# Q, K and softmax sums in four 64x64 quadrants on two PSUM banks, in a kernel of convolution, attention and experts

## The chip, the cores and the metric

The kernel runs on one core of a Trainium2 chip. A core has five engines that each work through their own instructions in order and wait for one another by semaphores: TensorE (PE, matrix products; its weight loads are shown apart as PEld), VectorE (DVE), ScalarE (ACT), GpSimd (POOL) and SyncE (SP, which issues most transfers). Matrix products go to PSUM, a small memory of eight banks of 2 KB in each of 128 partitions; ScalarE and VectorE carry them from there to SBUF.

The metric is the device time of one execution in microseconds (us). Before the change three runs took 1254.31 to 1254.89 us, median 1254.82.

## The reference, cut to what matters

Two layers on an input of 2 images, 256 channels, 56 x 56 pixels (N = 3136 tokens each). The first is a linear non-local convolution. The second is a transformer block on the tokens, all in float32:

```python
qkv = x @ W_attn                              # x: layer-normed tokens, C = 256
q, k, v = split(qkv)                          # 4 heads of 64
att = q @ k.T / 8, causal                     # per head, 3136 x 3136
att = softmax(att)
y = att @ v
t = t + y @ W_proj
t = t + experts(layernorm(t))                 # top 2 of 8 experts, 256 -> 512 -> 256
```

The change lies in the causal attention: in how Q and K are made, in how the rows of exponentials are summed for the softmax, and in when other work is put between the attention's steps.

## The kernel before

The program first does the convolution (to about 95 us), then the attention of both images (batches) in one long list of steps (to about 843 us), then the experts.

**Steps.** A step (`attend`, L707) belongs to a batch b, a block i of W = 448 queries (seven blocks), a head pair hp (two pairs, hp 0 first) and a chunk j of 128 keys. `scores` (L779) makes the products of keys and queries, transposed: keys in partitions, queries in columns, a 64x64 quadrant of the array for each half of the chunk and each head of the pair, into a tile `sc` of two banks, one for each head. ScalarE writes the exponentials to a tile `st` (L808; five buffers), VectorE multiplies the chunks that the causal mask cuts (L811) and adds `st` to the accumulator `acc` (L822 for a group's first two steps, L827 after). `values` (L832) runs three steps later (`LAG`) and adds the products with V to the output tile `yp`, two banks, a single buffer. Chunks that the mask cuts have fewer columns; they alternate with whole ones, so a group in block 0 has only narrow steps, block 1 ends on a narrow one, later blocks end on a whole one.

In each turn of the loop at L929 the order on TensorE is: the values of step n - 3, then the scores of step n; but where step n - 3 is the first of its group, its values come after the scores (`late`), so that the one output tile can be emptied. When a group's last values are done, ScalarE copies the output tile (L862) and GpSimd adds its two halves into `qT` (L863).

**Visits.** Three turns after a group's last step (in the turn in which its last values run) there is a visit (L930), ahead of that turn's values. `visit` (L2141) runs pieces that need the full 128x128 array: for hp 0, the Q and K products of the next segment of tokens (`query_key`, L607: two pairs of heads, Q and K, two matmuls of 128x512 each, then a ScalarE copy, L621), projections of finished tokens (`products`, `project_out`, L671), and a transposed tile of normed tokens (`transpose`, L591) of the segment after that; for hp 1 the V products of the next segment and further transposes. Segments have 512 tokens, the last two 384 and 192. These pieces take their PSUM tiles in turn (`bank`, L523) from two single banks (`pm`) and the two score tiles. After them `sum_rows` (L866) sums the accumulator over the keys with a matrix of ones, in four column groups of 32 (128x32 mode, 224 columns each), into a single bank; ScalarE copies the result (L881), four small DMAs on SP's queue write it to memory and one reads it back spread over partitions. Four steps later VectorE takes the reciprocal (`invert`, L892), it goes to memory and back as a broadcast, and six steps after that VectorE scales the output (`scale`, L907).

**Side work.** Between steps, `between` (L2162) pulls one piece of queued work a step (`pull`, L1970): layer-norm statistics of finished tokens (`closer`, L700), then the routing of batch 0's tokens to experts and their scattering, mostly small VectorE operations and GpSimd's indirect transfers. Nothing reorders this: the lists are written out in the program's order (`manual_schedule`, L2113), so each engine's queue is what the loop above emits.

**Score tiles.** `psc` has two buffers of two banks, called A and B here. Every score takes the next one; a score n + 2 thus waits until the exponential of score n has read its tile.

Of the kernel before, what the change touches and what calls it, by code (L numbers as in the profile page):

```python
# [28 lines left out]
def conv_attn_moe_kernel(  # L29
# [481 lines left out]
    def layer1(nm, general):  # L511

        with ExitStack() as whole:
# [20 lines left out]

            def centre_gate(place):

                gp = place("gp", (P, 512))
                gpc = gp[:, :E]
                for c in range(NH):
                    nc.tensor.matmul(gpc, ones, gw[:, c], start=(c == 0), stop=(c == NH - 1))  # L540
                for c in range(NH):
                    nc.vector.scalar_tensor_tensor(gwc[:, c], gpc, -1.0 / C, gw[:, c], ALU.mult, ALU.add)
                    nc.vector.tensor_copy(
                        wv[:, c, :, HS:], gwc[:, c].rearrange("p (h e) -> p h e", h=HEADS)
                    )
# [24 lines left out]
            def project_qkv(b, qT, kT, v, px):  # L570
# [51 lines left out]

                def value(s, n):
# [43 lines left out]
                return xs, qks, vs  # L667
# [30 lines left out]
            unclosed = [NCH] * B  # L698

            def closer(b, first, m, k):  # L700

                for n in range(first, first + m):
                    stats(b, n, 1, k, bg, f"o{nm}{b}")
                    unclosed[b] -= 1
                    yield True

            def attend(qT, kT, v, fst, fs, psc, py, open_batch, visit, between, clock, later, finished):  # L707
# [158 lines left out]
                def sum_rows(b, hp, i):  # L866
                    yh = qT[:, hp, i * W : (i + 1) * W]
                    r = (b * NH + hp) * NB + i
                    sn = f"{nm}{b}_{hp}_{i}"
                    acc = accs[b, hp, i]  # L870
                    summed.add((b, hp, i))
                    sp = bank(f"sp_{b}_{hp}_{i}")

                    flat = acc.rearrange("p a w -> p (a w)")
                    for g in range(4):
                        nc.tensor.matmul(  # L876
                            sp[g * 32 : (g + 1) * 32, : W // 2], ones[:, :32],
                            flat[:, g * W // 2 : (g + 1) * W // 2], start=True, stop=True,
                        )
                    line = fs.tile([P, W], F32, tag="rb", bufs=3, name=f"line_{sn}")  # L880
                    nc.scalar.copy(line[:, : W // 2], sp[:, : W // 2])  # L881
                    halves = sum_d[r].rearrange("a (h w) -> (a h) w", h=2)
                    for g in range(4):
                        nc.sync.dma_start(
                            out=halves[g : g + 1], in_=line[g * 32 : g * 32 + 1, : W // 2]
                        )
                    nc.sync.dma_start(
                        out=sums[:, r], in_=sum_d[r].rearrange("a (p f) -> (a p) f", p=HS)
                    )
                    later.append((clock[0] + 4, invert, b, hp, i, yh))  # L890

                def invert(b, hp, i, yh):  # L892
# [12 lines left out]
                    later.append((clock[0] + 6, partial(scale, rb), b, hp, i, yh))  # L905

                def scale(rb, b, hp, i, yh):  # L907
                    nc.vector.tensor_tensor(yh, yh, rb, ALU.mult)
                    later.append((clock[0] + 2, hand_on, b, hp, i, yh))
# [4 lines left out]
                def due(now):  # L914
                    while later and (now is None or later[0][0] <= now):
                        _, task, b, hp, i, yh = later.pop(0)
                        task(b, hp, i, yh)
                        later.sort(key=lambda e: e[0])

# [9 lines left out]
                for n in range(len(steps) + LAG):  # L929
                    if n in visits:  # L930
                        visit(*visits[n])
                        b, i, hp = visits[n]
                        if i >= 0 and visits[n] != final:
                            sum_rows(b, hp, i)
                        aligned()
                    if n + 1 < len(steps) and n > LAG and steps[n][2] == 0 and steps[n - LAG - 1][2] == 0 and steps[n - LAG - 1][4]:
                        turn_rows(*steps[n][:2])
                    if n < len(steps):
                        b, i = steps[n][:2]
                        if n == 0 or steps[n - 1][0] != b:  # L940
                            open_batch(b)
                        between(b, i, ends[b, i] - n, (steps[n][3] + 1) * P > i * W + 1)
# [5 lines left out]
                    if n >= LAG and not late:  # L948
                        values(n - LAG)
                    if n < len(steps):  # L950
# [3 lines left out]
                sum_rows(final[0], final[2], final[1])  # L954
# [1118 lines left out]
            if general:  # L2073
                centre_gate(bank)
                fold_gate(bank, turn_gate(bank))
                for b in range(B):
                    xs, qks, vs = project_qkv(b, qT, kT, v, px)
# [8 lines left out]
            else:  # L2086
# [9 lines left out]
                def ahead(b, i, hp):  # L2096

                    xs, qks, vs = projections[b]
                    if i < 0:
                        return vs(0), xs(1)  # L2100
                    if i + 1 < NS:
                        if hp == 0:
                            return qks(i + 1), xs(i + 2)[:1]
                        after = projections[b + 1][0](0) if i + 2 == NS and b + 1 < B else []
                        return vs(i + 1), xs(i + 2)[1:] + after
                    if b + 1 == B:
                        return [], []
                    xs, qks, vs = projections[b + 1]
# [5 lines left out]
                xs, qks, vs = projections[0]  # L2114
# [26 lines left out]
                def visit(b, i, hp):  # L2141

                    now, then = ahead(b, i, hp)
# [12 lines left out]
                    for _ in range(2):  # L2156
# [3 lines left out]
                    ring.clear()  # L2160

                def between(b, i, left, cut):  # L2162
# [7 lines left out]
                    if not cut or i:  # L2170
# [262 lines left out]
```

## Time and profile before

| | |
|---|---|
| median of three runs | 1254.82 us |
| the profiled execution | 1272.23 us |
| its span, first to last instruction | 1270.5 us |
| granted TensorE clock, mean | 0.995 |
| TensorE busy | 1247.3 us |
| VectorE busy | 773.9 us |
| ScalarE busy | 613.1 us |
| GpSimd busy | 356.2 us |
| Q and K products (L613), TensorE | 88.2 us, 224 records |
| scores (L804) and values (L855), TensorE | 347.5 and 328.0 us |

How to read it: a float32 matmul shows as two records, each with a weight load. Busy time of TensorE includes the time in which a record's results still move through the array, so a busy TensorE is not one that streams columns all the time; where starts of successive records are known, their distance is the better measure. In a timeline a row is a run of like instructions: start in us from the span's start, length, engine, line, operation, output and inputs, shape, count, and in brackets the idle time before it and who ended it. "64*64" or "128*32" is the part of the array that a matmul uses. A row of the waits names who waited for whom, total us, times and longest.

### The profile page before, as it was taken

The numbers are of one execution on the slowest core, as the hardware profiler recorded it, in microseconds if no ns is written. First come the engines' busy times: TensorE is split into PE (matmuls) and PEld (weight loads), VectorE is DVE, ScalarE is ACT, GpSimd is POOL, SyncE is SP. The second block draws the span as 40 slices with busy tenths as digits, with TensorE's granted clock in tenths as the row PEclk, the third lists the DMA queues.
The fourth block names the chain that finished last, engine by engine and source line by source line (L and its number), as shares of the span: only waits on it lengthen the run. The fifth ranks groups of instructions, "written<-read, shape, count | busy, mean of one in ns | idle before, by whom it ended". The sixth has DMA issues, their size and how long they took to land.

```text
span 1270.5 us, 28742 instructions
## 1 busy us (share of the span) xinstructions
PE 1247.3 (98%) x10881; PEld 857.1 (67%) x10881; DVE 773.9 (61%) x1687; ACT 613.1 (48%) x1237; POOL 356.2 (28%) x318
## 2 busy tenths in 40 slices
PE   8999999999999999999999999999999999999998
PEld 8876655555454645655555543469888999899996
DVE  2683567566766575576677887785743433455664
ACT  0255555565656565455555655563332333344442
POOL 1103231110021104211112766100266112666651
PEclk9999999999999999999999999999999999999999
DMA  9995101000000000100000223641344343466654
GB/s 314 354 345 187 25 23 37 25 15 26 14 17 16 7 20 17 36 21 14 9 16 25 71 67 110 202 136 61 101 135 151 101 114 101 142 200 200 212 164 125
DMA packets 118723, 125.66 MB, mean 99 GB/s; under 512 B 27223, under 2 KB 108488, under 8 KB 118578
## 3 DMA queue, kind: packets, MB, share of 16 engines
q1 hardware_dynamic: 107922, 97.19, 25.3%
q0 software_dynamic: 9840, 25.67, 6.0%
q8 instruction: 90, 1.47, 0.5%
q10 hardware_dynamic: 816, 0.88, 0.2%
q14 instruction: 55, 0.45, 0.1%
HBM read 62.06 MB, written 61.05 MB: 97 GB/s over the span
## 4 chain that ended last, share of the span: by engine, by line
PE 91%; DVE 4%; DMA 1%; issue 1%; ACT 1%; SPq 0%; DVEq 0%; ACTq 0%
PE sc_f L804 19%; PE yp_f L855 18%; PE ht_f L1637 14%; PE yp_f L1656 14%; PE qk_f L613 7%; PE v_f L628 4%; PE pp_f L682 3%; PE cp L410 3%; PE gram L317 2%; DVE acc_f L827 2%; PE tp_f L1614 2%; PE sp_f L876 1%; PE xp_f L599 1%; PE yo_f L1883 1%; DMA w1s_f<-in_w_dram 0%
## 5 line engine op out<-in xcount | busy, mean ns | idle before, releaser
L808 ACT ACTIVATE st_f<-sc_f 128x896 f32<-128x896 f32 (+5 forms) x400 | 330.7, 838 | 198.0 <-PE sc_f L804 178.9
L827 DVE TENSOR_TENSOR acc_f<-acc_f,st_f 128x896 f32<-128x896 f32 (+6 forms) x344 | 344.5, 1002 | 118.9 <-ACT st_f L808 109.1
L804 PE MATMUL sc_f<-qT_f,kT_f 64*64 64x448 f32 (+5 forms) x3136 | 347.5, 499 | 0.3 <-ACT st_f L808 0.3
L855 PE MATMUL yp_f<-st_f,v_f 64*64 64x448 f32 (+5 forms) x2928 | 328.0, 510 | 4.1 <-ACT acc_f L862 2.5
L804 PEld LDWEIGHTS sc_f<-qT_f,kT_f 64*64 64x64 f32 x3136 | 144.8, 133 | 128.9 <-issue 106.2
L1646 ACT ACTIVATE g_f<-ht_f,b1b 128x128 f32<-128x128 f32 x408 | 116.6, 371 | 227.3 <-PE ht_f L1637 123.4
L855 PEld LDWEIGHTS yp_f<-st_f,v_f 64*64 64x64 f32 x2928 | 125.1, 133 | 132.2 <-issue 99.3
L1637 PE MATMUL ht_f<-xT_f,w_f 128*128 128x128 f32 x1600 | 196.9, 276 | 5.2 <-issue 5.2
L1637 PEld LDWEIGHTS ht_f<-xT_f,w_f 128*128 128x128 f32 x1600 | 193.8, 192 | 9.1 <-issue 4.6
L1501 POOL DMA_INDIRECT x_slots<-xr_f,idx x100 | 120.4, 1204 | 147.0 <-DVE xr_f L1499 77.6
L863 POOL TENSOR_TENSOR qT_f<-acc_f 128x448 f32<-128x448 f32 x26 | 29.6, 1140 | 406.3 <-ACT acc_f L862 406.3
L1625 DVE COPY w_f<-w1s_f 128x1024 f32 x102 | 72.7, 713 | 90.0 <-PE ht_f L1637 34.2
L584 POOL TENSOR_SCALAR xn_f<-t 128x256 f32<-128x256 f32 (+1 forms) x50 | 82.4, 1655 | 129.4 <-DVE t L185 43.6
L1677 POOL DMA_INDIRECT y_tokens<-ys_f,to_f x57 | 59.2, 1038 | 125.2 <-DVE ys_f L1666 102.9
L613 PE MATMUL qk_f<-px_f,wat 128*128 128x512 f32 (+2 forms) x224 | 88.2, 546 | 0.6 <-ACT px_f L605 0.6
L1666 DVE TENSOR_TENSOR ys_f<-yp_f,kT_f 128x128 f32<-128x128 f32 x102 | 29.5, 289 | 92.3 <-PE yp_f L1656 69.5
L613 PEld LDWEIGHTS qk_f<-px_f,wat 128*128 128x128 f32 x224 | 40.6, 190 | 46.3 <-issue 41.7
L1656 PE MATMUL yp_f<-px_f,g_f 128*128 x204 | 62.3, 387 | 1.6 <-issue 1.6
L1656 PE MATMUL yp_f<-kT_f,g_f 128*128 x204 | 62.1, 386 | 0.0
L1656 PE MATMUL yp_f<-v_f,g_f 128*128 x204 | 61.8, 385 | 0.0
L1656 PE MATMUL yp_f<-w2s_f,g_f 128*128 x204 | 61.6, 384 | 0.0
L1834 POOL DMA_INDIRECT y_f<-y_slots,idx x50 | 55.5, 1110 | 17.1 <-issue 17.1
(299 smaller groups left out, 1302.4 us busy)
## 6 DMA issues: line engine op xcount, KB each, us to landing
x_slots<-fill SPq DMA_DIRECT2D x1, 8190.0 KB
xb_f<-x_slots SPq DMA_DIRECT2D x60, 130.0 KB
x_slots<-fill SPq DMA_DIRECT2D x1, 7296.0 KB
y_slots<-ys_f SPq DMA_DIRECT2D x57, 128.0 KB
kept<-t SPq DMA_DIRECT2D x2, 3200.0 KB
x<-in_x_dram SPq DMA_DIRECT2D x14, 448.0 KB
rb_f<-inverses SPq DMA_DIRECT2D x56, 112.0 KB
y_f<-y_tokens SPq DMA_DIRECT2D x23, 256.0 KB
```

The source lines that it names most:

```text
L584: nc.gpsimd.tensor_scalar(xn[:k, a], ts[b][:k, n + a, :C], ts[b][:k, n + a, MEAN : MEAN + 1], ts[b][:k, n + a, RSTD : RSTD + 1], ALU.subtr ...
L613: nc.tensor.matmul(ps[:, :w], wat[:, c, d0 : d0 + P], px[:, s % 2, c, :w], start=(c == 0), stop=(c == NH - 1),)
L804: nc.tensor.matmul(to, left, right, start=True, stop=True)
L808: nc.scalar.activation(st[rows, :, c0:], ps[rows, :, c0:W], AF.Exp, scale=SCALE)
L827: nc.vector.tensor_tensor(acc[rows, :, c0:], acc[rows, :, c0:], st[rows, :, c0:], ALU.add)
L855: nc.tensor.matmul(to, left, right, start=first, stop=end)
L1501: s = nc.gpsimd.indirect_dma_start(out=xds[b], out_offset=bass.IndirectOffsetOnAxis(ap=idxs[b][:kk, k, n : n + 1], axis=0), in_=xr[:kk], i ...
L1625: nc.vector.tensor_copy(w, w1s[:, :, bass.ds(e, 1), :].rearrange("p c e h -> p c (e h)"))
L1637: nc.tensor.matmul(ht[:, k, :], w[:, c, k * P : (k + 1) * P], xT[:, c, :], start=(c == 0), stop=(c == NH - 1),)
L1646: nc.scalar.activation(g[:, k, :], ht[:, k, :], AF.Gelu, bias=b1bs[b][:, k, i : i + 1])
L1656: nc.tensor.matmul(yp[:, :C], g[:, k, :], w2s[k][:, bass.ds(e, 1), :].rearrange("p e d -> p (e d)"), start=(k == 0), stop=(k == KH - 1),)
L1677: s = nc.gpsimd.indirect_dma_start(out=y_tokens, out_offset=bass.IndirectOffsetOnAxis(ap=to[:, n % GB : n % GB + 1], axis=0), in_=ys, in_o ...
```

## The change

- `quarters` replaces `query_key` in the visits of hp 0 in blocks 0 to 5 of both batches (twelve visits): each product's 128 contraction rows and 128 output rows are split in halves, four 64x64 matmuls for each. The two row halves of the contraction go to two banks. ScalarE copies the first bank to `qT` or `kT`, VectorE then adds the second bank to it. The first segment of each batch keeps `query_key`.
- `two_banks` gives the two banks: for the first three of the four products the next score tile, for the last the two single banks.
- `sum_quarters` replaces `sum_rows` in all groups but the last: four 64x64 matmuls of 448 columns, again on two banks, copied by ScalarE and added by VectorE; two line DMAs in place of four. In visits of hp 1 it uses the single banks, in visits of hp 0 a score tile.
- It runs after the last values of its group, not before them; the copy of the output tile therefore goes to a tile of the `st` ring and not to the accumulator.
- The visits of hp 0 hold no transposes any more (the next visit of hp 1 makes both tiles) and projections only in block 5 and, in batch 1, while batch 0 has some left; visits of hp 1 take up to four projections.
- Side work: `between` keeps an account (`spare`) of VectorE's time: each step adds what the step leaves free (`room`), each piece takes off a price, and a piece is pulled only above a floor. At the end of a visit `make_room` adds 2 us to the account and pulls pieces while it lasts.
- In the last block the scaling comes nine steps after the reciprocal, not six.

```diff
+            def two_banks(name, own):
+                if own:
+                    return [pm.tile([P, 512], F32, tag="m", name=f"{name}{x}_{nm}") for x in range(2)]
+                ps = score_banks[0].tile([P, 2, 512], F32, tag="sc", name=f"{name}_{nm}")
+                return [ps[:, 0], ps[:, 1]]
...
+                def quarters(s):
+                    first, end = SEGS[s]
+                    w = end - first
+                    for turn in range(2 * NH):
+                        which, hp = turn % 2, turn // 2
+                        d0 = which * C + hp * P
+                        halves = two_banks(f"qk4_{b}_{s}_{which}_{hp}", turn + 1 == 2 * NH)
+                        for c in range(NH):
+                            for r in range(2):
+                                rows = slice(r * HS, (r + 1) * HS)
+                                for o in range(0, P, HS):
+                                    nc.tensor.matmul(
+                                        halves[r][o : o + HS, :w],
+                                        wat[rows, c, d0 + o : d0 + o + HS],
+                                        px[rows, s % 2, c, :w],
+                                        start=(c == 0), stop=(c == NH - 1),
+                                    )
+                        to = (kT[hp] if which else qT[:, hp])[:, first:end]
+                        nc.scalar.copy(to, halves[0][:, :w])
+                        nc.vector.tensor_tensor(to, to, halves[1][:, :w], ALU.add)
...
+                def sum_quarters(b, hp, i):
+                    acc = accs[b, hp, i]
+                    sp = two_banks(f"sp_{b}_{hp}_{i}", hp > 0)
+                    for r in range(2):
+                        rows = slice(r * HS, (r + 1) * HS)
+                        for a in range(2):
+                            nc.tensor.matmul(
+                                sp[r][a * HS : (a + 1) * HS, :W], ones[rows, :HS], acc[rows, a],
+                                start=True, stop=True,
+                            )
+                    line = fs.tile([P, W], F32, tag="rb", bufs=3, name=f"line_{nm}{b}_{hp}_{i}")
+                    nc.scalar.copy(line, sp[0][:, :W])
+                    nc.vector.tensor_tensor(line, line, sp[1][:, :W], ALU.add)
+                    follow(b, hp, i, line, HS)
...
-                    later.append((clock[0] + 6, partial(scale, rb), b, hp, i, yh))
+                    loading = b == B - 1 and i == NB - 1
+                    later.append((clock[0] + (9 if loading else 6), partial(scale, rb), b, hp, i, yh))
...
+                def room(n):
+                    _, i, _, j, first, _, _ = steps[n]
+                    off = j * P - i * W
+                    width = W - max(0, off)
+                    return (
+                        2 * 0.75 * width / W
+                        - (0.42 if off > -P else 0)
+                        - (0 if first else 0.07 + 1.02 * width / W)
+                    )
...
                         visit(*visits[n])
-                        b, i, hp = visits[n]
-                        if i >= 0 and visits[n] != final:
-                            sum_rows(b, hp, i)
                         aligned()
...
                     if n >= LAG and not late:
                         values(n - LAG)
+                    if n in visits and visits[n][1] >= 0 and visits[n] != final:
+                        sum_quarters(visits[n][0], visits[n][2], visits[n][1])
                     if n < len(steps):
                         scores(n)
...
                 def visit(b, i, hp):
+                    if hp == 0 and 0 <= i and i + 1 < NS:
+                        projections[b][3](i + 1)
+                        if i + 2 == NS or b and not projected[b - 1]:
+                            for _ in range(2):
+                                products()
+                        return make_room()
...
-                    for _ in range(2):
+                    for _ in range(4 if hp and 0 <= i < NS - 2 else 2):
                         products()
...
+                def make_room():
+                    spare[0] = min(spare[0] + 2.0, 2.0)
+                    while spare[0] > 0.3:
+                        spare[0] -= 0.8 if placed[0] and not sent[0] else 0.5
+                        pull()
...
                     tick[0] += 1
-                    if not cut or i:
+                    spare[0] = min(spare[0], 1.0) + room
+                    sending = placed[0] and not sent[0]
+                    if spare[0] > (-0.9 if sending else -0.8):
+                        spare[0] -= 0.3 if sending else 0.35
                         pull()
```

## The prediction

> **What bounds the kernel now.** I read the page's busy table and its chain first.
>
> ```profile
> PE 1247.3 (98%) x10881; PEld 857.1 (67%) x10881; DVE 773.9 (61%) x1687; ACT 613.1 (48%) x1237; POOL 356.2 (28%) x318
> ...
> PE 91%; DVE 4%; DMA 1%; issue 1%; ACT 1%; SPq 0%; DVEq 0%; ACTq 0%
> ```
>
> TensorE is the path: 91% of the chain that ended last, and attention (about 100 to 843 us) is the stage that the change touches. So any matmul that waits there lengthens the kernel, and VectorE or ScalarE time counts only where a matmul waits for it. The timeline of TensorE around one visit (batch 0, block 2, head pair 0) shows what a visit costs; columns are start, time, engine, line, operation.
>
> ```profile
> 172.07 0.92 PE L804 MATMUL sc_f<-qT_f,kT_f 64*64 64x448 f32 x8
> 172.93 7.13 PE L613 MATMUL qk_f<-px_f,wat 128*128 128x512 f32 x16
> 179.90 0.60 PE L599 MATMUL xp_f<-ident,xn_f 128*128 128x128 f32 x4
> 180.43 0.59 PE L876 MATMUL sp_f<-acc_f,ones_t 128*32 128x224 f32 x8
> 180.95 0.98 PE L855 MATMUL yp_f<-st_f,v_f 64*64 64x448 f32 x8
> 181.75 1.29 PE L804 MATMUL sc_f<-qT_f,kT_f 64*64 64x448 f32 x9
> ```
>
> ScalarE and VectorE in the same stretch:
>
> ```profile
> 172.29 1.75 ACT L808 ACTIVATE st_f<-sc_f 128x896 f32<-128x896 f32 x2 [0.54 <-PE sc_f L804]
> 174.95 0.58 ACT L621 COPY qT_f<-qk_f 128x512 f32<-128x512 f32 x1 [0.91 <-PE qk_f L613]
> 176.67 0.59 ACT L621 COPY qT_f<-qk_f 128x512 f32<-128x512 f32 x1 [1.13 <-PE qk_f L613]
> ...
> 180.10 0.58 ACT L621 COPY kT_f<-qk_f 128x512 f32<-128x512 f32 x1 [1.13 <-PE qk_f L613]
> ...
> 181.08 0.34 ACT L881 COPY line_f<-sp_f 128x224 f32<-128x224 f32 x1
> 182.04 0.91 ACT L862 COPY acc_f<-yp_f 128x896 f32<-128x896 f32 x1 [0.61 <-PE yp_f L855]
> ```
>
> ```profile
> 174.39 1.08 DVE L822 TENSOR_TENSOR acc_f<-st_f,st_f 128x896 f32<-128x896 f32 x1
> ```
>
> Three readings. A Q or K product of 512 columns takes 1.72 us (copies at 174.95 and 176.67). A 64x64 set of eight records of 448 columns takes 0.76 us (scores at 181.75; the next set's records start at 182.51). A copy starts 0.20 us after its product's last column (180.10 against 179.90). Last, who keeps TensorE waiting in attention now (112 to 843 us; total, times, longest):
>
> ```profile
> PEld yp_f L855 <- ACT acc_f L862: 10.6, 26, 1.5
> ...
> PEld yp_f L855 <- DVE st_f L811: 7.4, 20, 1.6
> ...
> PEld sc_f L804 <- ACT st_f L808: 4.3, 12, 1.1
> ...
> PE yp_f L855 <- ACT acc_f L862: 2.5, 4, 0.7
> ```
>
> The weight loader idles, but the matmuls themselves lose 2.5 us to the output tile's copy and hardly anything else.
>
> **What the Trainium skill says.** "TensorEngine Tiling (Array Packing)", Key Properties: changing the tiling mode drains TensorE. The trace agrees: from 172.83 (172.07 + 0.76) to 180.95 are 8.12 us, of which products take 4 x 1.72 = 6.88, the transposes (a quarter of the columns of one product's four records) 0.43 and the sums (half the columns of a 0.76 set) 0.38. With 0.05 more on the first values (0.80 to 181.75 in place of 0.76), three mode changes cost 0.48 us. The same page, PSUM Pressure: different row tiles cannot use one PSUM bank at a time, hence the two banks; and PSUM Bottleneck: tiling does not speed evacuation. "TensorE: Matmul & The Clock Gate", Step-by-step: only weight loads are pulled ahead, matmuls stay in program order. The records here start in order; so a matmul that waits for a bank holds all behind it.
>
> **The change, part by part.**
>
> 1. *Q/K in quadrants.* 16 records of 128x128 become 64 of 64x64 with the same columns. Scores and values have this layout already and four such records take 0.38 us for 448 columns, so 0.43 for 512, what one full record takes. Streaming cost: 0. Twelve visits change (blocks 0 to 5 of two batches).
>
> 2. *Mode changes.* Nine of these visits (not block 5, where projections follow, nor batch 1's block 1) now have no 128-wide work: -0.48 each. The other 18 lose one change of three: -0.16.
>
> 3. *Sums in quadrants.* 27 blocks go from 0.38 to a full set of 0.76: +0.38. With part 2: 9 x (-0.10) + 18 x (+0.22) = +3.1 us. Bounds: if sums hide their own change wholly, +1; if quadrants save none for the 18, +6.
>
> 4. *Values ahead of sums.* The output tile is copied earlier than the next group's first values want it: -2.5 us (the last row above). The copy goes to a tile of the exponentials' ring of five in place of the accumulator; it is freed by GpSimd's add, which idled before 26 of 26 such adds (406.3 us of waiting), so I price it at 0; if GpSimd is late, an exponential four steps on waits.
>
> 5. *The score buffers: the main cost.* Two-bank tiles come from the two score tiles, A and B, except the last of the four products (and the sums of head pair 1), which has the two single banks. So products 1, 2, 3 take A, B, A; in these twelve visits the sums take B; then score n takes A and score n+1 takes B. B is free only when ScalarE has copied one half of the sums and VectorE, after it, has added the other. Clock from the last column before the visit, full width, in us: products to 6.88; last values to 7.64; sums to 8.40; score n to 9.16. ScalarE: fourth copy 7.08 to 7.67; output tile 7.84 to 8.75 (0.91); line copy of 448 columns 0.53 (between 0.34 for 224 and 0.58 for 512) 8.77 to 9.30. VectorE: line add 0.61 (between the PSUM adds L687, 264 columns, 0.429, and L418, 512 columns, 0.677) 9.33 to 9.94, and 0.06 to the semaphore: 10.0. Score n+1 waits from 9.16 to 10.0, **0.85 us**, and with it the first values and all exponentials behind. Nothing else can fill it. Block 1 has short last values (128 columns) and waits 1.2; block 0 has a short score n too and waits 1.8.
>    Side work that the new rule puts on VectorE between the fourth add and the line add comes on top. In batch 0 there is none that matters: 1.8 + 1.2 + 4 x 0.85 = 6.4. In batch 1 the built order shows it: four projection adds, three statistics pairs and a scaling at block 1 (line add done about 14.4, wanted 12.7), five small operations and a scaling at block 2 (10.7 against 9.16), four reductions and 200-column operations at 0.36 at block 3 (10.5), a like set at block 4: 1.8 + 1.7 + 1.6 + 1.4 + 1.1 + 0.9 = 8.5. Sum: **14.9 us**.
>
> 6. *Product 3 waits for A*, that is for product 1's copy and add. VectorE first adds the new group's first pair, in the timeline above from 1.46 after the visit began to 2.54, in most visits by 2.2. The add of product 1 ends at 2.9 to 3.2, wanted at 3.44: covered by little. For block 4 (384 columns, wanted 2.58, ready 2.88) it costs 0.3; for block 5 (192 columns, wanted 1.29) product 2 waits for the last exponential (1.15) and product 3 until about 2.7: 1.4; block 1 with late VectorE about 0.25. Twice each: **3.9 us**. If VectorE is 1 us later everywhere, 8 more.
>
> 7. *VectorE's load and the room rule.* 48 adds of halves (32 x 0.68, 8 x 0.55, 8 x 0.36 = 29 us) and 27 of lines (16.5) add 46 us to 774. VectorE stays under TensorE's time; the rule moves side work but at attention's end the built order has about as much of it left as before (two operations fewer). Price 0 beyond part 5. Two line DMAs on SP in place of four, later by some 2 us; the sums' return has four steps until the reciprocal: 0. The scaling of the last block waits nine steps in place of six; 0 to -1.
>
> Sum: 3.1 - 2.5 + 14.9 + 3.9 = **+19.4 us**. The profiled execution took 1272.2 us (span 1270.5), so 1291.6. The runs have a median of 1254.8, 17.4 below it; I carry the microseconds over: **1274**.
>
> **Rivals.** *A, faster:* VectorE-held waits were TensorE's time, and values first and the room rule remove them. If all that the weight loader idled for ScalarE's output copy, masks and exponentials (10.6 + 7.4 + 4.3, and 1.1 for accumulators) and the matmuls' own 3.9 (values behind the copy 2.5, masks 1.4) were lost, 27.3 us are to be had; 3.1 + 14.9 + 3.9 - 27.3 = -5.4, about 1249. It decides above 24.4 us. For it: that is what the rule is about. Against: the matmul rows show 3.9.
> *B, no stall:* the banks come free in time, or parts 5 and 6 only take up slack: 3.1 - 2.5, about 1255.
> *C, VectorE becomes the bound:* between 704 and 800 us it is busy 80 to 86%; with the added work masks and accumulations trail and the waits of parts 5 and 6 double: 1284 to 1300.
> *D, the quadrants of Q and K don't run side by side:* four times 6.9 us a visit, over 150 us more. Scores in the same layout speak against it.
>
> **How the numbers follow.** Likeliest (parts 1 to 7) 0.67, own range 1264 to 1284; A 0.12; B 0.09; C 0.10; D 0.02. The range 1254 to 1288 leaves out A, D and half of C. A measurement of this kernel tells 0.2% (2.5 us) from no change. Faster: A and a little of B, 0.13; same: most of B, 0.07; slower 0.80.
>
> **What would show it.** Right: idle of TensorE before a score tile's first matmul after the sums, released by VectorE's line add, 0.8 to 1.8 us in twelve places; smaller ones before product 3 at blocks 4 and 5; no gap between scores and the first quadrant product; quadrant products of 1.72 us. Wrong: that wait near zero, or many fewer idle microseconds in values and scores elsewhere than I allow, or a changed expert stage after 843 us, for which I allow nothing.

## The result and the profile after

| | before | after |
|---|---|---|
| median of six runs each (range) | 1254.78 us (1254.31 to 1255.47) | 1281.36 us (1279.79 to 1283.68) |
| profiled execution (span) | 1272.23 us (1270.5) | 1281.37 us (1279.5) |
| attention, first score to first expert product | 743.5 us | 767.2 us |
| experts, from there to the last matmul | 420.5 us | 404.8 us |

The kernel became slower by 26.6 us: the ratio is 1.0214, 95% interval 1.0204 to 1.0223. The two profiled executions differ by 9 us only, because the profile of before has a slow expert stage. That has nothing to do with the change: a second trace of the same kernel before, taken for the experiments, has an expert stage of 405.1 us and an attention of 741.0 us. So attention is what the traces are compared by, and it grew by 26.1 us (767.2 - 741.0; a second trace of after has 768.8: by 27.8).

The busy table and the chain of after:

```profile
PE 1248.9 (98%) x11457; PEld 853.5 (67%) x11457; DVE 821.4 (64%) x1762; ACT 621.4 (49%) x1237; POOL 334.0 (26%) x318
...
PE 94%; DVE 2%; ACT 2%; issue 1%; DMA 0%; SPq 0%; DVEq 0%; ACTq 0%
```

TensorE is the path as before. VectorE has 47.5 us more to do (821.4 against 773.9; 46 were forecast), but at 64% it is no bound over the whole. Who keeps TensorE waiting in attention is another matter (the waits of after from 112 to 865 us; total, times, longest):

```profile
PE sc_f L836 <- DVE line_f L924: 11.8, 11, 2.3
...
PE sc_f L836 <- ACT st_f L840: 2.3, 2, 1.1
...
PE pp_f L712 <- ACT kT_f L650: 1.5, 3, 0.7
...
PE qk_f L642 <- ACT st_f L840: 1.1, 5, 0.3
PE qk_f L642 <- DVE qT_f L651: 1.0, 2, 0.5
```

The first kind did not exist before: scores wait for VectorE's add of the two halves of the sums (L924), 11.8 us in eleven waits of the matmuls. The idle time of a row begins only where the record before it ends, and that is later than its last column, so the loss of streaming time, from start to start, is larger: 0.78 us where the row below says 0.61. The same visit as in the prediction (batch 0, block 2, head pair 0), timeline of all engines:

```profile
175.40 7.10 PE L642 MATMUL qk_f<-px_f,wat 64*64 64x512 f32 x64 [0.18 <-ACT st_f L840]
...
177.41 0.58 ACT L650 COPY qT_f<-qk_f 128x512 f32<-128x512 f32 x1 [1.15 <-PE qk_f L642]
...
179.13 0.58 ACT L650 COPY kT_f<-qk_f 128x512 f32<-128x512 f32 x1 [1.13 <-PE qk_f L642]
...
182.32 0.93 PE L887 MATMUL yp_f<-st_f,v_f 64*64 64x448 f32 x8
...
183.07 0.93 PE L918 MATMUL sp_f<-acc_f,ones_t 64*64 64x448 f32 x8
...
183.32 0.91 ACT L894 COPY both_f<-yp_f 128x896 f32<-128x896 f32 x1 [0.20 <-PE yp_f L887]
...
183.82 0.93 PE L836 MATMUL sc_f<-qT_f,kT_f 64*64 64x448 f32 x8
184.12 0.54 ACT L923 COPY line_f<-sp_f 128x448 f32<-128x448 f32 x1
...
184.69 0.62 DVE L924 TENSOR_TENSOR line_f<-line_f,sp_f 128x448 f32<-128x448 f32 x1 [0.32 <-ACT line_f L923]
...
185.36 0.22 PE L836 MATMUL sc_f<-fill 64*64 64x64 bf16 x2 [0.61 <-DVE line_f L924]
```

The copies come 1.72 us apart (177.41, 179.13), the price of a product before. Values, sums and the next score start 0.75 us apart, without a mode change between. Score n's columns end at 183.82 + 0.76 = 184.58. The next score can't start: ScalarE copies the output tile until 184.23, then the line until 184.66, VectorE adds until 185.31, and at 185.36 tile B is free. Lost: 0.78 us.

Block 0 is different. Score n+1 (four records of 64 columns) and VectorE's line add there, in batch 0:

```profile
119.10 0.27 PE L836 MATMUL sc_f<-qT_f,kT_f 64*64 64x64 f32 x2 [1.14 <-ACT st_f L840]
```

```profile
118.68 0.62 DVE L924 TENSOR_TENSOR line_f<-line_f,sp_f 128x448 f32<-128x448 f32 x1 [0.56 <-ACT line_f L923]
```

TensorE goes on at 119.10, while the line add runs until 119.30, so it did not wait for that add. What released it is the exponential of score n, which ScalarE could end only at 119.04, behind its copies of the output tile and of the line. Score n+1 thus did not take the tile of the sums here; the wait fits the tile of score n, and "every score takes the next one" does not hold in block 0. Batch 1 shows the same (the second of the two waits in the row above).

In the later blocks of batch 1 the wait is longer. The same place in its block 2, TensorE and then VectorE:

```profile
570.55 0.93 PE L836 MATMUL sc_f<-qT_f,kT_f 64*64 64x448 f32 x8
573.75 0.22 PE L836 MATMUL sc_f<-fill 64*64 64x64 bf16 x2 [2.27 <-DVE line_f L924]
```

```profile
569.88 0.69 DVE L651 TENSOR_TENSOR kT_f<-kT_f,qk_f 128x512 f32<-128x512 f32 x1 [1.00 <-ACT kT_f L650]
...
571.13 1.06 DVE L1230 TENSOR_TENSOR newton_y_f<-newton_y_f,red_f 128x25 f32<-128x25 f32 x1
...
572.35 0.82 DVE L961 TENSOR_TENSOR qT_f<-qT_f,rb_f 128x448 f32<-128x448 f32 x1
573.09 0.61 DVE L924 TENSOR_TENSOR line_f<-line_f,sp_f 128x448 f32<-128x448 f32 x1
```

Between the last product's add and the line add VectorE works off queued side work (L1230 among it) and a scaling. Its line add ends at 573.70, and TensorE stands still for 573.75 - 570.55 - 0.76 = 2.44 us.

Taken from the starts of records in this way (to about 0.02 us), the waits of score n+1 in blocks 0 to 5 are 1.36, 1.09, 0.79, 0.79, 0.79, 0.79 us in batch 0 and 1.36, 1.96, 2.46, 2.13, 1.47, 0.80 us in batch 1: 15.8 us in all. One more, of 0.82 us, stands in the last block of batch 1, where the sums of head pair 0 also take a score tile: 16.6 us. Of these, the two of block 0, 2.7 us together, end with ScalarE's exponential, the others with VectorE's line add. The waits of Q and K products and of the projections behind them come to about 8.2 us.

### The profile page after: what moved, and what is told of

Same layout as the page of the kernel before. It is cut to its first block, busy times and chain, and to the rows that moved or that the text cites. A ratio compares the mean times of both kernels' runs of the same rounds, so it can differ in the third digit from the quotient of the medians.

```text
span 1279.5 us, 29941 instructions
## 1 busy us (share of the span) xinstructions
PE 1248.9 (98%) x11457; PEld 853.5 (67%) x11457; DVE 821.4 (64%) x1762; ACT 621.4 (49%) x1237; POOL 334.0 (26%) x318
## 4 chain that ended last, share of the span: by engine, by line
PE 94%; DVE 2%; ACT 2%; issue 1%; DMA 0%; SPq 0%; DVEq 0%; ACTq 0%
PE yp_f L887 20%; PE sc_f L836 20%; PE ht_f L1701 14%; PE yp_f L1720 14%; PE qk_f L642 6%; PE v_f L658 4%; PE pp_f L712 4%; PE cp L410 3%; PE gram L317 2%; PE tp_f L1678 2%; PE qk_f L620 1%; ACT st_f L840 1%; PE sp_f L918 1%; PE xp_f L606 1%; PE yo_f L1947 1%
## 5 line engine op out<-in xcount | busy, mean ns | idle before, releaser
L836 PE MATMUL sc_f<-qT_f,kT_f 64*64 64x448 f32 (+5 forms) x3136 | 353.8, 499 | 8.6 <-DVE line_f L924 6.3
L887 PEld LDWEIGHTS yp_f<-st_f,v_f 64*64 64x64 f32 x2928 | 132.3, 133 | 122.4 <-issue 103.4
L1565 POOL DMA_INDIRECT x_slots<-xr_f,idx x100 | 114.2, 1142 | 146.9 <-DMA y_slots<-ys_f 62.4
L895 POOL TENSOR_TENSOR qT_f<-both_f 128x448 f32<-128x448 f32 x28 | 32.3, 1154 | 388.1 <-ACT both_f L894 388.0
L591 POOL TENSOR_SCALAR xn_f<-t 128x256 f32<-128x256 f32 (+1 forms) x50 | 65.3, 1313 | 251.7 <-PE xp_f L606 161.5
L642 PE MATMUL qk_f<-px_f,wat 64*64 64x512 f32 (+2 forms) x768 | 74.4, 532 | 2.7 <-ACT st_f L840 1.1
L1898 POOL DMA_INDIRECT y_f<-y_slots,idx x50 | 56.8, 1137 | 17.3 <-issue 17.0
L642 PEld LDWEIGHTS qk_f<-px_f,wat 64*64 64x64 f32 x768 | 27.3, 132 | 49.5 <-issue 29.9
```

The costliest lines, as they stand in the source:

```text
L591: nc.gpsimd.tensor_scalar(xn[:k, a], ts[b][:k, n + a, :C], ts[b][:k, n + a, MEAN : MEAN + 1], ts[b][:k, n + a, RSTD : RSTD + 1], ALU.subtr ...
L642: nc.tensor.matmul(halves[r][o : o + HS, :w], wat[rows, c, d0 + o : d0 + o + HS], px[rows, s % 2, c, :w], start=(c == 0), stop=(c == NH - 1),)
L836: nc.tensor.matmul(to, left, right, start=True, stop=True)
L887: nc.tensor.matmul(to, left, right, start=first, stop=end)
L1565: s = nc.gpsimd.indirect_dma_start(out=xds[b], out_offset=bass.IndirectOffsetOnAxis(ap=idxs[b][:kk, k, n : n + 1], axis=0), in_=xr[:kk], i ...
```

## The experiments

**How they are read.** The first four ran on one chip, where the expert stage takes 420 to 422 us in every trace and the kernel before 1270.9 us (1266.95 to 1274.55). So each run is compared with the kernel before as it ran beside it, and attention lengths are given as well. "Left of the loss" is the median less that of before beside it; for the change itself it was 26.6. No run of the changed kernel on that chip is on record, and before scatters by 7.6 us there, so for e1 to e4 the attention lengths are the better guide. The other experiments come from two further chips, on both of which before takes 1254.7 us; f5 to f7 are set against f3 across these two. Attention of a run is compared with both traces of after (767.2 and 768.8), hence two figures. For before_again, the kernel before once more, an attention of 740 to 741 us was expected, or 743 as in its first trace; it took 741.0.

| run | attention, us | median, us | before there | ratio (95%) | left of the loss |
|---|---|---|---|---|---|
| after, first | 767.2 | 1281.36 | 1254.78 | 1.0214 (1.0204 to 1.0223) | 26.6 |
| e1_banks_swapped | 752.2 | 1278.91 | 1270.90 | 1.0060 (1.0036 to 1.0084) | 8.0 |
| e2_old_pulls | 764.7 | 1293.20 | 1270.90 | 1.0179 (1.0146 to 1.0212) | 22.3 |
| e3_qk_whole | 758.9 | 1289.64 | 1270.90 | 1.0147 (1.0111 to 1.0184) | 18.7 |
| e4_sums_old | 749.9 | 1281.58 | 1270.90 | 1.0083 (1.0057 to 1.0109) | 10.7 |
| after_again | 768.8 | 1284.89 | 1254.75 | 1.0236 (1.0222 to 1.0250) | 30.1 |
| f1_values_first | 742.9 | 1255.90 | 1254.75 | 1.0011 (1.0003 to 1.0020) | 1.1 |
| f3_banks_in_order | 740.6 | 1255.05 | 1254.75 | 1.0004 (0.9996 to 1.0012) | 0.3 |
| f4_banks_old_pulls | 740.8 | 1255.12 | 1254.75 | 1.0006 (0.9998 to 1.0015) | 0.4 |
| before_again | 741.0 | 1254.72 | 1254.72 | 1.0001 (0.9993 to 1.0009) | 0.0 |
| f5_sums_all_quadrants | 743.3 | 1256.85 | 1254.72 | 1.0018 (1.0011 to 1.0024) | 2.1 |
| f6_sums_score_tile | 753.2 | 1267.64 | 1254.72 | 1.0101 (1.0086 to 1.0117) | 12.9 |
| f7_products_score_tiles | 743.7 | 1258.40 | 1254.72 | 1.0035 (1.0021 to 1.0048) | 3.7 |

### Taking parts of the change back

**e1_banks_swapped**: sums always on the two single banks, all four products on score tiles.

```diff
-halves = two_banks(f"qk4_{b}_{s}_{which}_{hp}", turn + 1 == 2 * NH)
+halves = two_banks(f"qk4_{b}_{s}_{which}_{hp}", False)
...
-sp = two_banks(f"sp_{b}_{hp}_{i}", hp > 0)
+sp = two_banks(f"sp_{b}_{hp}_{i}", True)
```

> The changed kernel with one thing exchanged: all four Q/K products take score tiles, the sums always take the two single banks. Theory (score n+1 waits for VectorE's line add because the sums sit in its tile): the waits after the sums, 15.8 us in twelve visits and 0.8 in the last block, go; product 3 waits as before. 1281.4 - 16 = about 1265 us (1262 to 1269), and no wait of a score for L924. Rival (the loss is the quadrant sums' own streaming, or VectorE's load): under 4 us are gained, 1277 or more.

Attention fell by 15.0 us (16.6 against the second trace of after), and the loss from 26.6 to 8.0 us. All the work is still done, the sums and both adds too; only the buffers differ. The timeline of TensorE at the same visit:

```profile
182.03 1.29 PE L836 MATMUL sc_f<-qT_f,kT_f 64*64 64x448 f32 x9
182.79 0.19 PE L836 MATMUL sc_f<-fill 64*64 64x64 bf16 x1
```

The second score's records now start 0.76 us after the first's (182.79): no wait. In block 0 score n+1 now waits 0.25 us by the row, for the add of the last product, where it waited 1.14. So the waits after the sums are real, they hang on where the sums are put, and they are most of the loss. The absolute time that was expected can't be held against a chip with another expert stage.

**e2_old_pulls**: side work by the old rule, one piece a step.

```diff
-    spare[0] = min(spare[0] + 2.0, 2.0)
-    while spare[0] > 0.3:
-        spare[0] -= 0.8 if placed[0] and not sent[0] else 0.5
-        pull()
+    return
...
-    spare[0] = min(spare[0], 1.0) + room
-    sending = placed[0] and not sent[0]
-    if spare[0] > (-0.9 if sending else -0.8):
-        spare[0] -= 0.3 if sending else 0.35
+    if not cut or i:
         pull()
```

> The changed kernel with the old rule for side work: one piece a step unless a block-0 step is cut, none at the end of a visit. Theory: only what batch 1 waits beyond batch 0 after the sums (10.2 against 5.6 us) goes, 1276 to 1278 us. Rival 1 (the new rule is the main loss, VectorE trails): 1262 or less. Rival 2 (the new rule saves waits elsewhere): 1283 or more.

Attention fell by 2.5 to 4.2 us, the loss by 4.3 us, though its interval is wide. The waits after the sums in batch 1 went from 1.36, 1.96, 2.46, 2.13, 1.47, 0.80 to 1.36, 0.83, 0.80, 0.79, 0.80, 0.79 us: most of what they had over 0.8 from block 1 on is side work in VectorE's queue. That is 4.8 us less; some of it comes back as new waits for masks (0.3 to 0.7 us) and for a projection's bank (1.1 us).

**e3_qk_whole**: Q and K as whole 128x128 products; sums in quadrants as in after.

```diff
-projections[b][3](i + 1)
+ring.append(0)
+for piece in projections[b][1](i + 1):
+    piece()
+ring.clear()
```

> The changed kernel with Q and K products in 128x128 form again, in the four tiles by turns; sums in quadrants stay. Theory: waits inside the products (about 6 us) and some of batch 1's waits go, three mode changes a visit come back (nine visits, 0.33 each more than now, sums being in quadrants), the wait of score n+1 stays: 1274 to 1279 us. Rival (Q and K in quadrants are slow by themselves): 1266 or less.

Attention fell by 8.3 to 10 us, the loss by 7.9 us: more than expected. The waits of the products and projections, about 8.2 us, are gone. But the waits of score n+1 in blocks 2 to 4 of batch 1 are down to 0.8 us as well (from 2.46, 2.13 and 1.47), and with smaller gains in blocks 0 and 1 that is some 4 us: without the adds of the products VectorE stands idle before the line add. About 2 us of mode changes come back, two in each of nine visits. So this run doesn't show the waits of Q and K alone.

**e4_sums_old**: the sums in four column groups on one bank, after the last values.

```diff
-sum_quarters(visits[n][0], visits[n][2], visits[n][1])
+sum_rows(visits[n][0], visits[n][2], visits[n][1])()
```

> The changed kernel with the sums in four column groups on one single bank again, after the last values; Q and K in quadrants stay. Theory: the waits after the sums (16.6 us) go, 27 sums stream 0.38 us less (10.3), nine visits get two mode changes (2.9) and eighteen one more (2.9): 1281.4 - 21 = about 1260 us (1257 to 1264). Rival (waits inside the products and the pull rule are the loss): 1274 or more.

Attention fell by 17.3 to 19 us, at the lower end of what was expected; the loss fell by 15.9 us. The expectation counted one mode change coming back for eighteen sums; as these now stand between values and scores, both in quadrants, it is two. Three sums also wait for ScalarE's copy of the last product (0.5 to 0.6 us each by the rows). e3 and e4 overlap, since e3 shortened waits after the sums too; they don't cut the loss into two clean parts.

### Building the change up with other banks

**after_again** is the changed kernel once more, beside the next three, with no edit.

> The changed kernel once more, so that it stands on one chip with the others. Attention (first score to first expert product in the trace) 767 us as in its first trace, 23 to 24 more than the kernel before (743.5); the whole by as much slower, 1.7 to 2.2%, if nothing outside attention differs.

Attention took 768.8 us and the ratio is 1.0236, a little above what was expected. The runs of the changed kernel spread over some 4 us on each chip (1281.2 to 1285.4 here), those of before beside it over 2; that isn't explained here.

**f1_values_first**: the kernel before, with only the order of last values and sums changed.

```diff
                     if n in visits:
                         visit(*visits[n])
-                        b, i, hp = visits[n]
-                        if i >= 0 and visits[n] != final:
-                            sum_rows(b, hp, i)
                         aligned()
...
                     if n >= LAG and not late:
                         values(n - LAG)
+                    if n in visits and visits[n][1] >= 0 and visits[n] != final:
+                        sum_rows(visits[n][0], visits[n][2], visits[n][1])
```

> The kernel before with one part of the change: the last values ahead of the sums. Theory: only the first values' wait for the output tile goes, about 2.5 us (2 in attention, 741). Rival (the copy's tile in the exponentials' ring holds ScalarE up, or the wait returns elsewhere): 743.5 or more, no change.

No gain: 1.1 us slower, with an interval that leaves out a gain of the 2.5 us that part 4 counted on. The waits show what became of it. Before (second trace, 100 to 845 us):

```profile
PE yp_f L855 <- ACT acc_f L862: 1.7, 3, 0.6
```

and f1:

```profile
PE yp_f L855 <- ACT both_f L862: 0.3, 2, 0.2
```

The wait for the output tile's copy did go (1.7 to 0.3 us). But the new order has a price. The timeline of TensorE in f1 at the visit that the prediction shows of before (batch 0, block 2):

```profile
173.58 7.13 PE L613 MATMUL qk_f<-px_f,wat 128*128 128x512 f32 x16
...
181.08 0.98 PE L855 MATMUL yp_f<-st_f,v_f 64*64 64x448 f32 x8
181.99 0.58 PE L876 MATMUL sp_f<-acc_f,ones_t 128*32 128x224 f32 x8
182.51 1.34 PE L804 MATMUL sc_f<-qT_f,kT_f 64*64 64x448 f32 x10
```

Before, the values and the score behind the sums have the same mode, 64x64: a visit has three mode changes (to 128x128, to 128x32, to 64x64). Here the values stand between the 128x128 work and the sums, and there are four. From the first product to the score the same matmuls take 8.93 us (182.51 - 173.58) where they took 8.82 (181.75 - 172.93): 0.11 more. Over all 27 such places f1 takes 3.9 us more (207.5 against 203.5 us in the second trace of before; 0.11 in each of 19, 0.21 to 0.25 in the eight of blocks 0 and 1, where the last values are short). Attention as a whole grew by 1.9 us only (742.9 - 741.0), so values first gained about 2.0 us elsewhere (one trace each), near the 2.5 of part 4, and the new order cost more than that. In the changed kernel this price doesn't arise, as its sums are in 64x64 mode themselves. That the mode change is what costs the 0.11 us is read from the order of the rows; f5 below gives it about the same price.

**f3_banks_in_order**: the change with other buffers. The first of the four products takes the single banks, which nobody has used for long, the others the score tiles; sums take the single banks; quadrant sums only in visits of hp 0 without open projections (eight by the trace, where nine were meant: block 0 of batch 1 keeps its column groups), and block 5 has whole Q and K products.

```diff
-halves = two_banks(f"qk4_{b}_{s}_{which}_{hp}", turn + 1 == 2 * NH)
+halves = two_banks(f"qk4_{b}_{s}_{which}_{hp}", turn == 0)
...
-sp = two_banks(f"sp_{b}_{hp}_{i}", hp > 0)
+sp = two_banks(f"sp_{b}_{hp}_{i}", True)
...
-visit(*visits[n])
+alone = visit(*visits[n])
...
-sum_quarters(visits[n][0], visits[n][2], visits[n][1])
+if alone:
+    sum_quarters(visits[n][0], visits[n][2], visits[n][1])
+else:
+    sum_rows(visits[n][0], visits[n][2], visits[n][1])()
...
-projections[b][3](i + 1)
-if i + 2 == NS or b and not projected[b - 1]:
+more = i + 2 == NS or b and not projected[b - 1]
+if i + 2 < NS:
+    projections[b][3](i + 1)
+else:
+    ring.append(0)
+    for piece in projections[b][1](i + 1):
+        piece()
+if more:
     for _ in range(2):
         products()
-return make_room()
+ring.clear()
+make_room()
+return not more
```

> The changed kernel with the tiles in another order: the first quadrant product takes the two single banks, the other three the score tiles, the sums the single banks; block 5 has whole Q and K products, and sums are in quadrants only in the nine visits without 128-wide work. Theory (all that is lost are waits for tiles, and the mode account of the prediction holds): nine visits gain 0.10 each, values first 2.5; attention 740 to 742 us, the whole 0.1 to 0.4% faster than the kernel before. Rival (what the swapped banks left, 8.7 us, is load on VectorE and ScalarE): 748 or more.

Attention is as expected (740.6 us), the time is not: the same as before, and not 0.1 to 0.4% faster. VectorE still has 808 us of work (777 in the second trace of before) and all the room rule's pulls, and TensorE waits for it four times only, 1.0 us in all by the rows. So the quadrants of Q and K, their adds and VectorE's load cost nothing that shows. The expected gain of 3.4 us left one term out: eighteen of the sums in column groups stand behind 128-wide work with the values between, so each has one mode change more than before, as in f1. At the 0.13 us that f5 gives for one that is 2.3 us, about what values first gained there.

**f4_banks_old_pulls**: f3 with the edit of e2.

> The same with the old rule for side work (one piece a step). Theory: with no bank that hangs on VectorE behind side work the rule hardly matters, within 1.5 us of the run with the new rule. Rival 1 (the rule saves waits for masks and accumulations): 3 us or more slower than that run. Rival 2 (the rule by itself costs): 3 us or more faster.

Within 0.1 us of f3 (0.2 in attention). So the rule for side work matters only where a bank hangs on VectorE.

**f5_sums_all_quadrants**: f3 with quadrant sums in all 27 places, 19 more (the edits of f5 to f7 are shown against f3).

```diff
-if alone:
+if True:
```

> The run with the tiles in order, but with the sums in quadrants in all 27 groups, on the single banks. Theory (prediction, parts 2 and 3: +0.38 for a sum, -0.16 for the mode change saved): 18 visits at 0.22, 4 us longer than that run (3 to 5.5). Rival (the sums hide in the mode changes): within 1.5 us of it.

1.8 us above f3's difference to its kernel before (2.1 - 0.3), and 2.7 in attention; 4 were expected. 19 sums at 0.38 us more each are 7.2 us. With values first each of them saves two mode changes, into 128x32 and back to 64x64, and not the one that the expectation counted. So two are worth 0.23 to 0.28 us, and one 0.12 to 0.14, not 0.16.

**f6_sums_score_tile**: f3 with its eight quadrant sums in a score tile.

```diff
-sp = two_banks(f"sp_{b}_{hp}_{i}", True)
+sp = two_banks(f"sp_{b}_{hp}_{i}", False)
```

> The run with the tiles in order, but the nine quadrant sums go to a score tile as in the changed kernel; nothing else moves. Theory: score n+1 waits for VectorE's line add in nine visits as in the changed kernel's trace, 12 us longer than that run (10 to 14). Rival (TensorE's time is bounded by something else and makes the wait up): under 4 us.

12.6 us more, as expected, from one word: the same instructions, other banks. By the starts of records about 9 us of it are waits of score n+1; in block 0 they end with the exponential, as in after. In blocks 0 and 1 of batch 0 score n waits as well, 0.5 to 0.6 us by the rows, for the add of a product. The timeline of TensorE at block 2 of batch 1, f6 and then f3:

```profile
560.30 0.98 PE L836 MATMUL sc_f<-qT_f,kT_f 64*64 64x448 f32 x8
563.41 0.22 PE L836 MATMUL sc_f<-fill 64*64 64x64 bf16 x2 [2.12 <-DVE line_f L924]
```

```profile
555.11 1.29 PE L836 MATMUL sc_f<-qT_f,kT_f 64*64 64x448 f32 x9
555.87 0.19 PE L836 MATMUL sc_f<-fill 64*64 64x64 bf16 x1
```

From one score to the next 3.11 us with the score tile, 0.76 with the single banks.

**f7_products_score_tiles**: f3 with all four products in score tiles, the first of them in A.

```diff
-halves = two_banks(f"qk4_{b}_{s}_{which}_{hp}", turn == 0)
+halves = two_banks(f"qk4_{b}_{s}_{which}_{hp}", False)
```

> The run with the tiles in order, but all four quadrant products take score tiles, A first. Theory (a term that the prediction left out): product 1 follows the last score at once and waits until the exponential of the score before has read tile A, 0.2 to 0.5 us in nine visits, 3.4 us longer than that run (2.5 to 4.5). Rival: no wait, within 1 us of it.

3.4 us more, as expected. The timeline of TensorE at block 2 of batch 0 shows where; f7 and then f3:

```profile
171.72 0.92 PE L836 MATMUL sc_f<-qT_f,kT_f 64*64 64x448 f32 x6
172.82 7.10 PE L642 MATMUL qk_f<-px_f,wat 64*64 64x512 f32 x64 [0.18 <-ACT st_f L840]
```

```profile
171.58 0.92 PE L836 MATMUL sc_f<-qT_f,kT_f 64*64 64x448 f32 x6
172.28 7.09 PE L642 MATMUL qk_f<-px_f,wat 64*64 64x512 f32 x64
```

The first product starts 1.10 us after the last score's records with a score tile, 0.70 with the single banks: 0.40 us of waiting for the exponential that still reads A. The row of the waits gives only 0.18 for it.

## Why the prediction was right and where it failed

Right in sign, in the likeliest case and in its main cost; 7.2 us short of the median (26.6 against 19.4). By its own steps, in us:

| part | forecast | measured | by |
|---|---|---|---|
| 1 to 4: streaming, mode changes, sums, values first | +0.6 | about +2.1 to 2.3 | f5 against before |
| 5: score n+1 waits for the line add | 14.9 | 16.6, of it 2.7 for an exponential | starts of records in after |
| 6: products wait for their tile | 3.9 | about 8.2, with projections | starts of records in after |
| 7: VectorE's load and room rule | 0 beyond part 5 | none that shows | f3 and f4 |
| sum | 19.4 | about 27 | attention of after: 26.1 to 27.8 |

**Part 1** held: products 1.72 us apart, in quadrants as whole, and a copy of 0.58 us as before, with VectorE's add of 0.69 on top. That one bank would not have done for both row halves, no run here tests.

**Parts 2 and 3** counted the mode changes rightly: none is left between scores, products, values and sums in nine visits, and one of three went in the other 18. Their price was too high. In the nine, f3's score comes 8.37 us after the first product, where before took 8.82; without the transposes (0.43) and with 0.38 more for the sums, the three changes were worth 0.40 us and not 0.48. With 0.11 to 0.14 for one (f1 and f5), the 45 saved changes bring 5 to 6.3 us of the 7.2 booked, so that parts 2 and 3 cost 4 to 5 us and not 3.1, within the bounds that were given.

**Part 4** was nearly right: 2.5 us were booked, and f1 shows about 2.0 gained outside of the 27 places that it reorders. f1 as a whole was slower only because its sums, in 128x32 mode behind the values, need a fourth mode change; the changed kernel doesn't have it. Parts 1 to 4 then come to 10.3 for the sums, less 5.9 (45 changes at 0.13) and 2.0: +2.4, against 2.1 to 2.3 measured in f5. These terms aren't measured one by one in the changed kernel.

**Part 5** held in place and size, and in mechanism in ten of its twelve places. The 0.85 us of the clock worked out was 0.78 to 0.79 in the trace; block 1 of batch 0 lost 1.09 rather than 1.2. Block 0 lost 1.36 rather than 1.8, and by another way: score n+1 waited for the exponential of score n, which stood in ScalarE's queue behind the copies of output tile and line. This still hangs on the sums' bank, as in e1 nothing waits for that exponential. In batch 1 the built order had shown that side work comes between, with 1.7, 1.6, 1.4, 1.1 for blocks 1 to 4; they were 1.96, 2.46, 2.13, 1.47. In f6, which moves nothing but the sums' banks, those of blocks 2 to 4 come back with 2.3, 2.0 and 1.5. Block 6 of batch 1, with its 0.82, was left out of the list of places.

**Part 6** is the step that was mis-sized most, 3.9 against about 8.2 us. It asked when product 3 finds A free, and worked that out a little too dear: at 512 and 384 columns product 3 did not wait at all. It did not ask the same of product 1, which takes A as well, from the exponential of the score before last: 0.16 to 0.54 us in each of ten visits, about 3.6 us together, and 0.6 in block 5. Nor of the projections behind product 4, which need one of its two single banks: 0.58 us in block 5 of each batch and 0.84 in block 1 of batch 1. In block 5 the waits of products 2 and 3 were 0.29 and 0.69 us, 1.0 a visit where 1.4 were forecast. f7 shows the product 1 term alone (3.4 us). The whole of part 6 rests on the starts of records in after; e3 agrees with it, but mixes in shorter waits after the sums.

**Part 7** held as far as the runs go: 32 us more of work on VectorE cost nothing that shows where no bank waited for it (f3, 808.4 against 776.6), and the rule for side work nothing either (f4). In the change itself the rule costs the 2.5 to 4.3 us of e2, but that is the surplus of part 5 in batch 1, which was priced there.

**Rivals.** A fell: as its counter-argument said, only the waits in the rows of the matmuls were to win. TensorE's idle time ahead of values went from 4.1 us (3.1 in the second trace) to 0.3, too little to outweigh parts 5 and 6. B is what f3 and f4 show, with other banks than those of the change: no stall, the time of before. C was right only in small: VectorE is 64% busy, yet in four visits of batch 1 its queue sets the end of the wait. D fell at the first copies.

**The carry-over** of microseconds from a profile 17.4 us above the median was right, as the surplus lies outside of the change: 15.4 us in the expert stage, 2.5 in attention. The sign "a changed expert stage" in the list of what would show it wrong did appear (404.8 against 420.5), but the second trace of before has 405.1, so it belongs to the execution and not to the change.

## What to carry to other kernels

Before a result is spread over two banks that two engines empty one after the other, follow each bank forward to the next matmul that takes it: the price is that matmul's wait (0.8 to 2.5 us here), with all that TensorE has behind it, and the queue of the last engine, side work and all, is part of it. Ask it of every user of the tile, the first one and those behind the last one too, and give the late-emptied result the buffer that is wanted last; the choice of banks alone was worth 12.6 us. When matmuls are put in another order to save a wait, count the mode changes of both orders: f1 gained about 2 us and paid 3.9.

## What the runs showed of the hardware

- A float32 product of 128x512 from 256 rows takes 1.72 us whole or in quadrants of 64x64, so splitting neither gains nor loses streaming time; it adds an emptying step (ScalarE 0.58 us, then VectorE 0.69).
- One change of TensorE's mode was worth 0.11 to 0.14 us: 0.11 where f1 has one more at a visit, 0.23 to 0.28 for two (f5 against f3), 0.40 for three (f3 against before, block 2).
- The expert stage of one and the same program took 405.1 us in one trace and 420.5 in another, with gaps of TensorE for which the profile names no releaser; on the chip of the first four experiments all traces had about 420 and the kernel before took 1270.9 us, on the others 1254.7. The cause wasn't looked for. It is why absolute times of different chips were not compared.
- Why the changed kernel itself varies between 1279.8 and 1285.4 us stays open.
